# Three uses of split fp32 products in a one-core graph network: the seventh gated product, the queries, and a block of keys

## The chip, the core and the metric

The kernel runs on one core of a Trainium2 chip. A core has a matrix engine (TensorE, PE in the profile, with PEld for the loading of its stationary operand), a vector engine (VectorE, DVE), a scalar engine (ScalarE, ACT), a general engine (GpSimd, POOL) and a queue for transfers (SyncE, SP). The metric is the device time of one execution in microseconds. The kernel before takes 2311.24 us (median of three runs, 2310.18 to 2312.17).

## What is computed

The reference takes 1024 nodes of 512 features, 16384 edges sorted by target, and a condition of 16 x 256 rows. After a layer norm and a ReLU there are a batch norm, one graph convolution, four layers, a second graph convolution, and two residual sums. One layer is:

```python
a = _attn(_ln(h, ln2_w[i], ln2_b[i]), cond, Wq[i], Wk[i], Wv[i], Wo[i])
h = h + a
u = _ln(h, ln3_w[i], ln3_b[i]) @ geglu_w[i] + geglu_b[i]
val, gate = jnp.split(u, 2, axis=-1)
f = val * jax.nn.gelu(gate, approximate=False)
h = h + f @ ffo_w[i] + ffo_b[i]
```

The attention has 16 groups of 64 nodes and 8 heads of 64, with keys and values from the condition. The gated product maps 512 features to 2 x 2048, the last product 2048 back to 512. All is fp32.

## The kernel before

**Two ways of an fp32 product.** A *plain* fp32 matmul of 128 x 128 by 512 columns stands in the trace as two records. A *twelve-bit* product splits each factor into a high part, a low part and a third part (their difference), in tiles of the type fp32r; three matmuls, high x high, low x low and third x third, give the same product together, with one pass over the bank between the second and the third (multiply by 1 + 2^-12). The class `Twelve` (L366, scale at L377, copy at L382 and L384) does this for keys and values: `begin` multiplies high and low and scales, `end` multiplies the third parts and copies the bank out. `staggered` begins each unit before it ends the one before, and calls functions `beside` the units for other work.

**Seven products in place of eight.** Queries and gated products go by a scheme in which a 2 x 2 block product takes seven block products and sums of blocks. `sums_of_a` and `sums_of_b` make the sums of the factors. For the queries (`QueryQuad`, L297) all seven are plain; their sums are `weight_sums` on POOL and `sum_first` on DVE or POOL, and the sums of the results are passes of DVE (L1274). The gated product has four rounds r of four blocks c. Round 0 (`Quad`) is plain. Rounds 1 to 3 are twelve *chunks* per layer: `Chunk.steps` is a generator that a loop advances, and six of its seven products are twelve-bit (L1091). The seventh (i = 2, L1154) is two plain matmuls onto the bank of product 4.

**Splitting in the gated stage.** The right factors (rows) are split once per layer by `all_parts`, in 24 steps that `fill` places between the plain products of round 0. The left factors (weights of a chunk) arrive in two tiles, `gxa` (four blocks of 256 columns, a slot) and `gxb`, become sums on POOL (`sums`, L1071), then split: `gha`/`ghb` on ACT (L1031), `gla`/`glb` on DVE (L1033), `gsa`/`gsb` on POOL (L1037). Chunk c's last steps run among the first of chunk c + 1.

**The output stage.** `Output.unit` multiplies f (stored to memory and loaded again by `fetch`) with the last weights in 16 units, two rows of weights blocks each, two passes s over the same eight weight units. `split` splits f (ACT L314, DVE L315 and L317), `split_w` the weights (L1211, L1214, L1218), `fetch_w` loads them. In pass s = 0 blocks 0, 1, 4, 5 of h are completed, in s = 1 the others.

**Order.** Instructions go to each engine's queue by a planner that follows the order of writing. `pin` keeps the written order among pinned instructions, `in_order(engine)` chains all of one engine's instructions in a block one behind the other, `issue_after` puts a block behind one instruction, and `waiting_for(ins, engine)` makes an engine's instructions wait for `ins`. Tiles come from pools: 36 `slots` of 128 x 1024 fp32, eight banks of PSUM, six `accs`; an instruction that first writes a tile waits until a buffer is free.

**The start.** Behind a branch (`tc.If`) the root of the degrees is taken on DVE, and PE does two plain blocks of keys (`begin("k1", c, ...)`, L353) before the aggregation `agg_in` (L752), whose low rows are `hs_low` (L795). Two blocks of keys of group 1 are thus already there in layer 0.

## Time and profile before

| what | value |
|---|---|
| median of the runs | 2311.24 us (2310.18 to 2312.17) |
| profiled execution | 2311.66 us, its span 2309.9 us |
| PE busy | 2285.7 us, 99% |
| DVE, ACT, POOL busy | 1684.5 (73%), 1093.9 (47%), 646.3 us (28%) |
| granted clock of PE | 0.999 |
| layer 0, round 0 of the gated product, from 413.6 us | 34.7 us, DVE busy 32.0, POOL 4.9 |
| layer 0, the twelve chunks, from 448.3 us | 120.1 us, DVE busy 97.9, POOL 75.1 |
| layer 0, output stage, from 568.4 us | 87.1 us, DVE busy 80.7 |
| layer 1, first keys to the first scores, from 655.5 us | 49.5 us, DVE busy 31.8 |

A row of the timeline is: start, length of the group, engine, line, operation, what is written from what, shapes, count, and in brackets how long the engine stood idle before and for whom. PE's records overlap their neighbours, so the price of a matmul is the distance of the starts, not the length.

### The profile page before, as it was taken

The page shows a single profiled execution, that of the slowest core. Times are in us where ns is not written, and L with a number is a line of the kernel's source. Part 1 is how long each engine was busy: PE and PEld are TensorE (multiplying, and loading weights), DVE is VectorE, ACT ScalarE, POOL GpSimd, SP SyncE. Part 2 cuts the span into 40 slices and gives each one's busy share as a digit, 9 for nine tenths or more (in the row PEclk, how much of TensorE's full clock was granted, in tenths as well). Part 3 has the DMA queues.
Part 4 walks back from the last instruction along what each step waited for, and adds up shares of the span by engine and source line. Part 5 has one row for each costly group of instructions (what it writes and reads, how often), then busy time and mean ns, then how long its engine had stood idle before and what let it go on. Part 6 is the DMA issues. An engine that isn't in the chain of part 4 may idle for free. (4 is left out here: it accounts for less than half of the span.)

```text
span 2309.9 us, 33555 instructions
## 1 busy us (share of the span) xinstructions
PE 2285.7 (99%) x12236; PEld 1710.5 (74%) x12236; DVE 1684.5 (73%) x3111; ACT 1093.9 (47%) x2117; POOL 646.3 (28%) x575
## 2 busy tenths in 40 slices
PE   8999999999999999999999999999999999999999
PEld 4667887577877888477886888567786888667787
DVE  9876556888976556978987554988887555888965
ACT  7544445455344445455344444555335445545421
POOL 1121213274031224175022222256021123146201
PEclk9999999999999999999999999999999999999999
DMA  7042220244521101144522111033531111033551
GB/s 214 11 142 70 69 73 24 73 128 153 175 73 47 56 19 37 46 120 132 187 92 74 37 37 37 28 110 119 188 132 60 33 56 37 6 114 116 178 177 60
DMA packets 160493, 204.37 MB, mean 88 GB/s; under 512 B 11241, under 2 KB 101681, under 8 KB 160321
## 3 DMA queue, kind: packets, MB, share of 16 engines
q1 hardware_dynamic: 158224, 196.72, 26.6%
q0 software_dynamic: 1376, 4.30, 0.5%
q8 instruction: 101, 1.65, 0.3%
q10 hardware_dynamic: 720, 1.11, 0.1%
q14 instruction: 72, 0.58, 0.1%
HBM read 151.75 MB, written 50.34 MB: 87 GB/s over the span
## 5 line engine op out<-in xcount | busy, mean ns | idle before, releaser
L320 POOL TENSOR_TENSOR as_c<-ah_c,al_c 128x512 fp32r<-128x512 f32 x128 | 199.5, 1587 | 923.9 <-DVE al_c L315 482.0
L1105 ACT ACTIVATE g<-g 128x512 f32<-128x512 f32 x192 | 112.9, 588 | 193.0 <-PE g L1091 193.0
L377 ACT ACTIVATE k<-k 128x512 f32<-128x512 f32 x124 | 72.2, 585 | 225.0 <-PE k L366 223.8
L1237 PE MATMUL fy<-bh_wff,ah_f 128*128 128x512 f32 x512 | 159.2, 392 | 0.0
L1237 PE MATMUL fx<-bs_wff,as_f 128*128 128x512 f32 x512 | 157.8, 389 | 0.5 <-DVE as_f L317 0.5
L1237 PE MATMUL fy<-bl_wff,al_f 128*128 128x512 f32 x512 | 157.8, 389 | 0.0
L382 DVE COPY kT<-k 128x512 f32<-128x512 f32 x54 | 37.2, 688 | 158.4 <-PE k L366 158.4
L314 ACT ACTIVATE ah_f<-fr 128x1024 fp32r<-128x1024 f32 x64 | 67.5, 1060 | 177.0 <-PE fy L1237 112.9
L366 PE MATMUL v<-bs_wv,as_c 128*128 128x512 f32 x508 | 138.4, 394 | 3.9 <-ACT v L377 3.9
L366 PE MATMUL v<-bh_wv,ah_c 128*128 128x512 f32 x508 | 140.8, 399 | 0.0
L847 ACT ACTIVATE pr<-sc,nmax 128x256 f32<-128x256 f32 x256 | 118.0, 474 | 47.6 <-DVE nmax L842 47.1
L366 PE MATMUL v<-bl_wv,al_c 128*128 128x512 f32 x508 | 136.5, 390 | 0.0
L1091 PE MATMUL g<-gr,gsa 128*128 128x512 f32 x384 | 136.2, 436 | 0.0
L366 PE MATMUL k<-ah_c,bh_wk 128*128 128x512 f32 x496 | 133.9, 392 | 0.0
L377 ACT ACTIVATE v<-v 128x512 f32<-128x512 f32 x127 | 75.0, 591 | 122.4 <-PE v L366 122.4
L366 PE MATMUL k<-al_c,bl_wk 128*128 128x512 f32 x496 | 132.6, 389 | 0.0
L366 PE MATMUL k<-as_c,bs_wk 128*128 128x512 f32 x496 | 131.5, 396 | 0.1
L1037 POOL TENSOR_TENSOR gsa<-gha,gla 128x512 fp32r<-128x512 f32 x88 | 112.3, 1297 | 64.0 <-DVE gla L1033 64.0
L1091 PE MATMUL g<-gr,gha 128*128 128x512 f32 x384 | 120.7, 395 | 0.0
L1091 PE MATMUL g<-gl,gla 128*128 128x512 f32 x384 | 118.6, 390 | 0.0
L366 PEld LDWEIGHTS v<-bs_wv,as_c 128*128 128x128 f32 x508 | 93.8, 189 | 27.7 <-ACT v L377 5.6
L366 PEld LDWEIGHTS v<-bh_wv,ah_c 128*128 128x128 f32 x508 | 92.6, 188 | 27.9 <-issue 9.2
(326 smaller groups left out, 5542.1 us busy)
## 6 DMA issues: line engine op xcount, KB each, us to landing
f_dram<-fT SPq DMA_DIRECT2D x128, 256.0 KB, 2.7
fr<-f_dram SPq DMA_DIRECT2D x64, 512.0 KB, 4.5
ct<-cond_dram SPq DMA_DIRECT2D x48, 512.0 KB, 4.3
wff<-in_L_gnn_ffo_w_dram SPq DMA_DIRECT2D x32, 512.0 KB, 5.9
gxb<-in_L_gnn_geglu_w_dram SPq DMA_DIRECT2D x96, 128.0 KB, 2.8
gxa<-in_L_gnn_geglu_w_dram SPq DMA_DIRECT2D x96, 128.0 KB, 2.8
cond<-in_L_gnn_cond_dram SPq DMA_DIRECT2D x32, 256.0 KB, 3.8
cond_dram<-ct SPq DMA_DIRECT2D x16, 512.0 KB, 3.3
```

Of the source, the lines that this page charges most:

```text
L314: nc.scalar.mul(twelve_bits(h), x, INWARD * TINY)
L320: nc.gpsimd.tensor_tensor(twelve_bits(s)[:, k, :], h[:, k, :], l[:, k, :], OP.subtract)
L366: pin(nc.tensor.matmul(self.bank, twelve_bits(left[k // 2])[:, k % 2, self.c * P:(self.c + 1) * P], twelve_bits(right[k // 2])[:, k % 2, : ...
L377: nc.scalar.mul(self.bank, self.bank, 1.0 + TINY)
L382: nc.vector.tensor_copy(self.to(), self.bank)
L847: nc.scalar.activation(pr3[:, a, :], ps3[:, a, :], AF.Exp, bias=nmax[:, a:a + 1], accum_out=tot[:, a:a + 1])
L1037: split_left.last = pin(t.tensor_tensor(s_at, h_at, l_at, OP.subtract))
L1091: pin(nc.tensor.matmul(to, self.part(i, which)[:, k, :], self.rights[i][which].bitcast(F32R)[:, k, :], start=start and k == 0, stop=stop a ...
L1105: pin(nc.scalar.mul(to, to, 1.0 + TINY))
L1237: pin(nc.tensor.matmul(to, twelve_bits(left[which][0])[:, k, b * P:(b + 1) * P], twelve_bits(right[which])[:, k, :], start=u == 0 and whic ...
```

## The change

The seventh product of a chunk becomes twelve-bit like the others: its left block (`x[2]`, 256 columns) and its right factor are split too, its result gets its own bank (`scale_onto(2, u2)`, `end(2)`), and the sum `u2` is made before. The queries become twelve-bit products over the whole 512 rows and columns, without the seven-product scheme, in two halves of the rows: `Rows` splits four normalised blocks, `QueryWeights` the weights, `queries` gives `Twelve` units. Of the keys of group 1 one block is begun behind the branch, not two. Beside these: two right factors (`BESIDE`) give their third part to POOL; POOL's subtractions of a chunk wait for the DVE pass on the next chunk's `gla`; three chunks are loaded ahead, not two; one unit of output weights is split before the output stage, not two; `wo` is split in steps between keys; f is stored by halves of the rows, so that h is completed in the order 0 to 7; 35 slots, not 36.

```diff
-    slots = ctx.enter_context(tc.tile_pool(name="slots", bufs=36))
+    slots = ctx.enter_context(tc.tile_pool(name="slots", bufs=35))
...
+    def three_halves(name):
+        return rows.tile([P, 3 * D // 2], F32, tag="gs2", name=name, bufs=2)
...
-    f_dram = dram.tile([2, DFF // P, P, 2, 256], F32, name="f_dram")
+    f_dram = dram.tile([2, DFF // P, P, 512], F32, name="f_dram")
...
-    for c in range(2):
-        begin("k1", c, raw_wk, raw_x[0, 1])
+    with waiting_for(rsqrt.first, mybir.EngineType.PE):
+        begin("k1", 0, raw_wk, raw_x[0, 1])
...
+        yield ([high[:, c, :] for c in range(HP)], [low[c // 2][:, c % 2, :] for c in range(HP)],
+               third)
...
+            yield
...
+            yield
...
-    SPLIT = (0, 5, 6, 4, 1, 3)
-    EARLY = (0, 1, 4, 6, 5, 3)
+    SPLIT = (0, 5, 6, 4, 1, 3, 2)
+    EARLY = (0, 1, 4, 6, 5, 3, 2)
+    BESIDE = (4, 6)
...
+    def right_beside(name, x, h, s):
+
+        low = slot(f"gl_{name}")
+        nc.scalar.mul(h.bitcast(F32R), x, INWARD / TINY)
+        less = [t512(f"gt_{name}_{k}") for k in range(2)]
+        for k in range(2):
+            nc.scalar.mul(less[k], h[:, k, :], TINY)
+        for k in range(2):
+            yield low
+            pin(nc.vector.scalar_tensor_tensor(low.bitcast(F32R)[:, k, :], x[:, k, :], 1.0 / TINY,
+                                               h[:, k, :], OP.mult, OP.subtract))
+            pin(nc.gpsimd.tensor_tensor(s.bitcast(F32R)[:, k, :], low[:, k, :], less[k],
+                                        OP.subtract))
+
...
-        pin(nc.scalar.mul(h.bitcast(F32R), x, INWARD * TINY))
-        yield
-        pin(nc.vector.scalar_tensor_tensor(l.bitcast(F32R), h, -1.0 / TINY, x, OP.mult, OP.add))
-        yield
+        yield pin(nc.scalar.mul(h.bitcast(F32R), x, INWARD * TINY))
+        split_left.low = pin(nc.vector.scalar_tensor_tensor(l.bitcast(F32R), h, -1.0 / TINY, x,
+                                                            OP.mult, OP.add))
+        yield split_left.low
...
-            if c % 2 == 0:
-                tag = ("row", "last")[c // 2]
-                Chunk.room = rows.tile([P, D], F32, tag=tag, name=f"gy_{self.n}")
-            self.last = columns_of(Chunk.room)[:, c % 2]
+            self.x.append(rows.tile([P, M], F32, tag="gy", name=f"gy_{self.n}", bufs=2))
...
             if low:
-                to = [t512(f"g{n}b_{self.n}") for n in "hls"]
+                last = three_halves(f"gs2_{self.n}")
+                all_to = [[t512(f"g{n}b_{self.n}") for n in "hls"],
+                          [last[:, i * M:(i + 1) * M] for i in range(3)]]
             else:
-                to = [flat(slot(f"g{n}a_{self.n}")) for n in "hls"]
-            self.parts[low] = [columns_of(t.bitcast(F32R)) for t in to]
-            yield from split_left(self.x[low], *to, t)
-
+                all_to = [[flat(slot(f"g{n}a_{self.n}")) for n in "hls"]]
+            flows = []
+            for i, to in enumerate(all_to, int(low)):
+                self.parts[i] = [columns_of(t.bitcast(F32R)) for t in to]
+                flows.append(split_left(self.x[i], *to, t))
+            for flow in flows:
+                next(flow)
+            yield
+            while flows:
+                flow = flows.pop(0)
+                if next(flow, None):
+                    flows.append(flow)
+                    yield
...
+            add(u2, d, u2)
             self.scale_onto(3, u3)
+            self.scale_onto(2, u2)
...
-            for k in range(2):
-                pin(nc.tensor.matmul(d, self.last[:, k, :], self.rights[2][:, k, :], start=False,
-                                     stop=k == 1, skip_group_check=True))
+            d = self.end(2)
...
-            add(d, d, u2)
...
+                nc.sync.dma_start(f_dram[s, self.r * KC + c], self.tiles[c][:, s, :])
...
+        def split(self, n, t=nc.vector):
...
+                self.f[n] = left_parts([self.raw.pop(n)], f"f_{self.l}_{n}", t)
...
-                    to = h[4 * (b // 2) + 2 * s + b % 2]
+                    to = h[4 * s + b]
...
+    class Rows:
+
+        def __init__(self, l, half, x):
+            self.x, self.n, self.parts = x, f"ln2_{l}_{half}", [[], [], []]
+
+        def high(self, i):
+            for n, part in zip("hls", self.parts):
+                part.append(slot(f"b{n}_{self.n}_{i}"))
+            nc.scalar.mul(twelve_bits(self.parts[0][i]), self.x[i], INWARD / TINY)
+
+        def low(self, i):
+            (h, l, _), x = (t[i] for t in self.parts), self.x[i]
+            for k in range(2):
+                nc.vector.scalar_tensor_tensor(twelve_bits(l)[:, k, :], x[:, k, :], 1.0 / TINY,
+                                               h[:, k, :], OP.mult, OP.subtract)
+
+        def third(self, i):
+            h, l, s = (t[i] for t in self.parts)
+            for k in range(2):
+                nc.vector.scalar_tensor_tensor(twelve_bits(s)[:, k, :], h[:, k, :], -TINY,
+                                               l[:, k, :], OP.mult, OP.add)
...
+    class QueryWeights:
+
+        def __init__(self, l, x):
+            high = four_wide(f"ah_wq_{l}")
+            self.x, self.l = x, l
+            self.parts = [[high[:, :2, :], high[:, 2:, :]], [], []]
+
+        def high(self, i):
+            for n, part in zip("ls", self.parts[1:]):
+                part.append(slot(f"a{n}_wq_{self.l}_{i}"))
+            nc.scalar.mul(twelve_bits(self.parts[0][i]), self.x[i], INWARD * TINY)
+
+        def rest(self, i):
+            (h, l, s), x = (t[i] for t in self.parts), self.x[i]
+            nc.vector.scalar_tensor_tensor(twelve_bits(l), h, -1.0 / TINY, x, OP.mult, OP.add)
+            for k in range(2):
+                nc.gpsimd.tensor_tensor(twelve_bits(s)[:, k, :], h[:, k, :], l[:, k, :],
+                                        OP.subtract)
+
+    def queries(l, half, wq, rows, by):
+
+        to = blocks_in(qTs, half, f"qT_{l}_{half}")
+        return [Twelve(f"q_{l}_{half}_{c}", wq.parts, c, rows.parts, to(c), by[c % 2])
+                for c in range(KC)]
...
+        wq = QueryWeights(l, wq)
...
         else:
-            scale_first(1, deviations(mv_first[1], "ln2_0_4"))
-            with waiting_for(scale_first.last, mybir.EngineType.Pool):
-                wq = weight_sums(wq, "wqs_0")
+            root = deviations(mv_first[1], "ln2_0_4")
+            for i in range(2):
+                wq.high(i)
+                with waiting_for(rsqrt.last, mybir.EngineType.Pool):
+                    wq.rest(i)
...
+        def split_first(i):
+            first_rows.high(i)
             with in_order(mybir.EngineType.DVE):
-                turn_first(l, half[1][:2], ((1, 1),))
+                first_rows.low(i)
+                if l:
+                    first_rows.third(i)
...
+        def split_wq(i):
+            wq.high(i)
+            with in_order(mybir.EngineType.DVE):
+                wq.rest(i)
+
+        def staggered_queries(half, rows, beside):
+            staggered(queries(l, half, wq, rows, (1, 0)), beside)
...
-                staggered(units, {1: lambda: first(0, 1), 2: lambda: first(2, 3), 4: turn_some,
-                                  6: lambda: to_scale[0](0, 1), 7: turn_more})
+                staggered(units, {0: lambda: split_wq(0), 1: lambda: first(0, 1),
+                                  2: lambda: first(2, 3), 3: lambda: split_wq(1), 4: turn_some,
+                                  5: lambda: split_first(0), 6: lambda: split_first(1),
+                                  7: lambda: to_scale[0](0, 1)})
+                staggered_queries(0, first_rows, {
+                    0: lambda: (to_scale[0](2, 3), turn_more(*half[1][:2])),
+                    1: lambda: (turn_more(*half[1][2:]), begin_more(), more_rows.high(0)),
+                    2: lambda: (finish_more(0), more_rows.high(1)),
+                    3: lambda: finish_more(1)})
...
-            staggered(units, {2: turn_some, len(units) - 1: lambda: turn_first(0, range(4, 8))})
-            sum_first(nc.gpsimd, 0)
-            sum_first(nc.gpsimd, 1)
+            with in_order(mybir.EngineType.Activation), in_order(mybir.EngineType.DVE):
+                staggered(units, {2: turn_some, 3: lambda: split_first(0),
+                                  4: lambda: (split_first(1), first_rows.third(0),
+                                              first_rows.third(1), scale_first(1, root))})
+                staggered_queries(0, first_rows, {
+                    1: lambda: (turn_more(*range(4, 8)), begin_more(), more_rows.high(0)),
+                    2: lambda: (finish_more(0), more_rows.high(1)),
+                    3: lambda: finish_more(1)})
...
+        split_cond(l, 1)
+        staggered_queries(1, more_rows, {})
...
+            wo_flow = out_parts(l, wo) if not g else iter(())
+            wo = next(wo_flow, wo)
...
-            k = keys(l, g + 1, wk, 2 if l == 0 and g == 0 else 0)
+            k = keys(l, g + 1, wk, 1 if l == 0 and g == 0 else 0)
...
+                next(wo_flow, None)
...
+                if i in BESIDE:
+                    flow = right_beside(name, x, high, mid)
+                    Chunk.rights[i] = high, next(flow), mid
+                    yield
+                    for _ in flow:
+                        yield
+                    continue
...
+        def begin_split(n, low, t=nc.gpsimd):
+            flow = ready[n].split_steps(low, t) if n < len(ready) else iter(())
+            next(flow, None)
+            return flow
+
+        first_chunk = []
+
+        def fill_first():
+            for flow in first_chunk.pop(0):
+                next(flow, None)
...
-                first_chunk = split_first()
-            q.rest((lambda: next(first_chunk.pop(0), None)) if c == KC - 1 else fill)
+                long, short = (begin_split(0, low) for low in (False, True))
+                first_chunk.extend([[parts], [long] * 3, [short], [short] * 4, [], []])
+            q.rest(fill_first if c == KC - 1 else fill)
...
+        def split_rest(short):
+            long = begin_split(0, False)
+            next(long, None)
+            with waiting_for(split_left.low, mybir.EngineType.Pool):
+                for flow in short, long:
+                    for _ in flow:
+                        pass
...
-                if n > 0:
+                if 0 < n < 5:
...
-                if before:
-                    chunk.split(True, nc.gpsimd)
+                for _ in islice(short, 2):
+                    pass
...
-                    split(0, False)
+                    split_rest(short)
                     load()
+                for _ in parts:
+                    pass
...
-                    output.split(0)
+                    with in_order(mybir.EngineType.Activation), in_order(mybir.EngineType.DVE), \
+                            in_order(mybir.EngineType.Pool):
+                        output.split(0, nc.gpsimd)
                     output.fetch(1)
...
-                    if step == 0 and n >= 0 and n % KC == 0:
-                        next(ahead)
...
+                short = begin_split(0, True)
+                if n == 0:
+                    next(ahead)
+        output.fetch_w(1)
         output.fetch_w(2)
-        output.fetch_w(3)
...
-            half = [0, 1, 4, 5], [2, 3, 6, 7]
+            half = range(4), range(4, 8)
...
-                output.fetch_w(n + 4)
+                output.fetch_w(n + 3)
```

160 lines of the change are left out of this document (41 added, 119 removed).

## Prediction

> **What bounds the kernel now.** I read the page first, then what TensorE (PE) waited for, then PE's timeline stage by stage, and last the other engines beside it.
>
> ```profile
> span 2309.9 us, 33555 instructions
> ...
> PE 2285.7 (99%) x12236; PEld 1710.5 (74%) x12236; DVE 1684.5 (73%) x3111; ACT 1093.9 (47%) x2117; POOL 646.3 (28%) x575
> ...
> PEclk9999999999999999999999999999999999999999
> ```
>
> PE is busy in 2285.7 of 2309.9 us, at full granted clock. Of the 24 us left these waits of PE (total, times, longest) are those that the change can touch:
>
> ```profile
> PE v L366 <- ACT v L377: 3.9, 4, 2.5
> ...
> PE begun_k L353 <- DVE v_deg L151: 1.7, 1, 1.7
> PE g L1091 <- DVE g L1109: 1.3, 4, 0.3
> ```
>
> The rest is the start, before the first matmul has data. So the time is what PE has to stream, plus any new idle. VectorE (DVE) at 73% is an average and says nothing of a stage. Two prices carry the sum, both from PE's timeline (start, length of the group, what, how many records):
>
> ```profile
> 145.84 1.88 PE L297 MATMUL qb<-ln2S,wqs 128*128 128x512 f32 x4
> ...
> 163.01 1.91 PE L201 MATMUL tr_cond<-ident,cond 128*128 128x128 f32 x16
> ...
> 470.04 1.88 PE L1154 MATMUL g<-ln3T,gy 128*128 128x512 f32 x4
> ...
> 479.97 1.88 PE L1154 MATMUL g<-ln3T,gy 128*128 128x512 f32 x4
> ...
> 655.52 1.07 PE L366 MATMUL k<-ah_c,bh_wk 128*128 128x512 f32 x4
> ...
> 665.49 1.07 PE L366 MATMUL v<-bh_wv,ah_c 128*128 128x512 f32 x4
> ```
>
> From 145.84 to 163.01 us ten query products of four records each ran back to back: 17.17 / 10 = 1.717 us for a product, which is two plain fp32 matmuls over 512 columns. From 655.52 to 665.49 eleven groups of four twelve-bit matmuls ran: 9.97 / 44 = 0.2266 us each. From one L1154 to the next is one gated chunk: 9.93 us.
>
> **The change part by part.**
>
> *Seventh gated product.* Per chunk two plain matmuls (1.717) become six twelve-bit ones (6 x 0.2266 = 1.360). PE saves 0.357 us per chunk; 3 rounds x 4 chunks x 4 layers = 48 chunks: -17.1 us. A chunk then takes 9.57 us, if the other engines keep up. One chunk of layer 0 on DVE, POOL and ScalarE (ACT), and each engine's busy time in it:
>
> ```profile
> 489.58 1.75 DVE L1033 SCALAR_TENSOR_TENSOR gla<-gha,gxa 128x1024 fp32r<-128x1024 f32 x1 [0.77 <-ACT gha L1031]
> ...
> 495.21 0.69 DVE L1109 SCALAR_TENSOR_TENSOR g<-g,gs 128x512 f32<-128x512 f32 x1
> ...
> 570.13 1.22 DVE L315 SCALAR_TENSOR_TENSOR al_f<-ah_f,fr 128x1024 fp32r<-128x1024 f32 x1
> ...
> 488.96 1.29 POOL L1037 TENSOR_TENSOR gsb<-ghb,glb 128x512 fp32r<-128x512 f32 x1 [1.96 <-DVE glb L1033]
> 491.41 2.55 POOL L1037 TENSOR_TENSOR gsa<-gha,gla 128x512 fp32r<-128x512 f32 x2 [1.16 <-DVE gla L1033]
> 493.92 0.74 POOL L1071 TENSOR_TENSOR gxa<-gxa,gxb 128x256 f32<-128x256 f32 x1
> 494.74 1.44 POOL L1071 TENSOR_TENSOR gxa<-gxa 128x256 f32<-128x256 f32 x2
> ...
> 498.43 1.04 ACT L1031 ACTIVATE gha<-gxa 128x1024 fp32r<-128x1024 f32 x1
> ...
> 489.90:499.80 9.90, 9.90 (x41) 7.51 (x40) 8.01 (x12) 6.25 (x11) 6.75 (x8) 1.00 0.35 106
> ...
> 413.60:448.30 34.70, 34.70 (x82) 14.72 (x80) 31.99 (x50) 16.39 (x23) 4.92 (x7) 1.00 0.23 69
> ```
>
> DVE gains one pass from a bank (0.69) and a 256-wide low part (0.4, estimated from half of a 512-wide pass). It loses a block: `gla` took 1.75 us where it began at 489.58 while POOL's `gsb` ran until 490.25; a 1024-wide pass of the same kind without POOL is 1.22 (`al_f`, in the output stage). The new order lets POOL start only behind it. So 8.01 + 1.1 - 0.5 = 8.6 of 9.57 us. A weight step (`wff`) is in that sum, which the last three chunks no longer have. POOL gains a 256-wide subtraction: 6.75 + 0.74 = 7.5 of 9.57; ACT gains some 0.4 on 6.25. No bound there by busy time.
>
> The right factor of the seventh product is split in the quads' stage (last row: 34.70 us, DVE busy 31.99, POOL 4.92). Two of the seven factors give their third part to POOL, so the steps between the products stay 24, and DVE's passes in them stay 24. Four POOL passes of 1.29 can block DVE there, 5.2 us at the very most, against 2.7 us idle; and the first chunk's third parts leave DVE for POOL, three passes, 2 us. I cost it at nothing; without that cover it is at most 0.5 us per layer. In the chunk that ends a layer the last product waits for a bank's pass with nothing between; PE waits there 0.3 us now (1.3 over four layers, above), and I leave it.
>
> *Queries.* Per layer 7 products x 2 x 1.717 = 24.0 us become 2 halves x 4 blocks x 12 x 0.2266 = 21.8: -2.3. What they need now comes out of a longer chain for each half of the rows: turned (ACT and DVE), high part (ACT), low and third parts (DVE). Layer 1:
>
> ```profile
> 668.22 1.91 PE L201 MATMUL tr_ln<-ident,xn_ln 128*128 128x128 f32 x16
> ...
> 668.86 2.65 DVE L812 TENSOR_SCALAR ln2T<-tr_ln,cols 128x128 f32<-128x128 f32 x8 [7.42 <-PE tr_ln L201]
> ...
> 675.40 0.16 DVE L1333 SCALAR_TENSOR_TENSOR less_ln<-mv,y_ln 128x4 f32<-128x4 f32 x1
> ...
> 672.05 0.63 ACT L377 ACTIVATE v<-v 128x512 f32<-128x512 f32 x1
> ...
> L314 ACT ACTIVATE ah_f<-fr 128x1024 fp32r<-128x1024 f32 x64 | 67.5, 1060 | 177.0 <-PE fy L1237 112.9
> ...
> 96.55 1.28 DVE L338 SCALAR_TENSOR_TENSOR bs_wk<-bh_wk,bl_wk 128x512 fp32r<-128x512 f32 x2
> ...
> 705.02 1.96 PE L835 MATMUL sc<-kT,qT 64*64 64x256 f32 x32
> ```
>
> PE's transposes end at 669.9 and ten groups of 0.907 follow: the first query starts at about 679.0. ACT has turned by 672.05; in its fixed order come two scales and two copies (0.6 each, as in that row) beside the two high parts (1.06 each, the mean of `ah_f` on the page): 677.2. DVE ends the second half's root at 675.6 and makes low and third parts, eight passes of 0.64 (as `bs_wk`): 680.7; PE wants the low ones from 679.9 to 680.8 and the third ones from 682.7. That fits, and the second half has seven groups, 6.3 us, of the first one before it. So -2.3 in each of layers 1 to 3, -6.8 (bounds: 0 to +1 us of idle in each). Layer 0 has less cover:
>
> ```profile
> 85.39 7.11 PE L353 MATMUL begun_k<-ct,wk 128*128 128x512 f32 x16 [1.71 <-DVE v_deg L151]
> 91.93 0.79 PE L752 MATMUL agg_in<-high,c 128*128 128x512 f32 x1
> ...
> 88.31 2.08 DVE L795 SCALAR_TENSOR_TENSOR hs_low<-hs_in,y_deg,high 128x512 fp32r<-128x512 f32 x3 [0.92 <-ACT high L794]
> ...
> 129.07 1.91 PE L201 MATMUL tr_ln<-ident,xn_ln 128*128 128x128 f32 x16
> ...
> 129.71 3.38 ACT L814 ACTIVATE ln2T<-tr_ln,cols 128x128 f32<-128x128 f32 x8 [0.26 <-PE tr_ln L201]
> ...
> 126.67 1.91 DVE L189 TENSOR_SCALAR xn_ln<-hall,mv_first,y_ln 128x512 f32<-128x512 f32 x4
> ```
>
> There five units stand before the queries, not eight. After the transposes (130.8) PE has seven groups, until 137.1. ACT turns until 133.1; behind two scales, a high part and a copy its second high part ends at 138.0: PE stops 0.5 us in the first query. DVE goes on with six passes of 0.64 and the four normalised blocks of the second half (1.91, put behind them now), so that their transposes end 0.7 late; its two copies and eight turning steps reach 148.1, a high part and a scale on ACT 149.8, where PE wants that scale at 148.6; the same again for the next block. Together 0.5 + 0.7 + 1.2 + 1.2, some 3.5 us of idle, estimated (0 to 5).
>
> *One begun block, not two.* From 85.39 eight records fewer, 3.4 us. The aggregation then wants its first low row, which DVE has at 88.31 + 0.7 = 89.0 where PE is free at 88.8: -3.2. The block comes back as twelve matmuls: +2.7. They stand between the first two scores of layer 0, in front of the place where PE lost the 2.5 us above (an ACT scale queued behind softmax work that DVE brought late); that cover takes most of it: -2.0 (0 to -2.5). The steps of `wo`'s split between the keys are the same instructions: nothing (or the other 1.4 us of that row). Layer 0 in sum: -2.3 + 3.5 - 3.2 + 2.7 - 2.0 = -1.3.
>
> *Output stage.* Only the first of eight units of weights is split before the stage, not two; the second has to be made during the first unit (24 x 0.2266 = 5.44 us):
>
> ```profile
> 568.05 1.02 PE L1237 MATMUL fy<-bh_wff,ah_f 128*128 128x512 f32 x2
> ...
> 569.47 0.75 DVE L1160 SCALAR_TENSOR_TENSOR fT<-g,gcols,g 128x512 f32<-128x512 f32 x1
> ...
> 572.53 0.68 DVE L1214 SCALAR_TENSOR_TENSOR bl_wff<-wff,bh_wff 128x512 fp32r<-128x512 f32 x1
> ...
> 574.58 0.69 DVE L1218 SCALAR_TENSOR_TENSOR bs_wff<-bh_wff,bl_wff 128x512 fp32r<-128x512 f32 x1
> ```
>
> Now DVE makes here, between the last `fT` and 575.3, the weights of the unit after next; then they are those of the next. The first matmul of the stage begins to stream when the last plain one is through, 568.46; unit 1 at 573.9, and it wants its last third part at 575.0. The chunk in front ends 1.3 us sooner after its gates, which brings DVE some 0.4 later against PE: 0.3 to 0.7 us of idle, four times, +2.0 (0 to +4). From there DVE has 5.1 us of work per 5.44 and gains. On SP the weight loads keep their place behind the last stores; `f` stored in rows of 512, not twice 256, and the other order of the blocks of `h` move no work.
>
> **Sum.** -17.1 - 6.8 - 1.3 + 2.0 = -23.2, against the profiled execution (2311.66 us; span 2309.9): 2288.5. The median of the runs shown is 0.4 below that execution: 2288.
>
> **The rivals.**
>
> *POOL's chain paces the chunk.* From one `gla` to the next the new order runs `gsb` 1.29, the new subtraction 0.74, `gsa` 2.55, three sums (493.92 to 496.18) 2.26, `gha` 1.04, `gla` 1.22: 9.1 us, some 9.4 with the hand-overs (0.08 us from 491.33 to 491.41), against 9.57. If `gla` is blocked again it is 10.0: eleven steps fall 4.7 us behind, of which 2.3 are cushion (`gsa` is ready that much before PE wants it). Four layers give back 4 x 2.4 = 10 us: 2298. For it speaks how near 9.4 is; against it that POOL stands idle before each `gsb` now. The Trainium skill, "SBUF — State Buffer", Who interferes with whom, has a DVE instruction with two SBUF inputs and a POOL one that reads SBUF exclude each other for the whole instruction. By that rule, with which 1.75 against 1.22 agrees, POOL too can be blocked by `glb`, and the chain is 10.0.
>
> *Slower: the split chain of the rows is not covered.* ACT's fixed order holds a query block's scale behind the turning and the high part of the next half. Per layer turning 3.4, two high parts 2.1 and four low passes 2.6 make 8.1 us; exposed once in each layer, 32 us less the 3.5 counted: 2317. The sign turns at (23.2 + 3.5) / 4 = 6.7 us per layer. Against it: nine microseconds of units stand in front in layers 1 to 3.
>
> *Every wait goes.* Layer 0 without idle and without the 2.5 (-5.3), the other 1.4 and the 1.3 gone, nothing lost in Output: -17.1 - 6.8 - 5.3 - 2.7 = -32: 2280.
>
> *PE waits for room instead* (35 slots, not 36, with three more held by the seventh factor and one more chunk loaded ahead): the 17.1 come back as waits, 2305. I count 34 slots held in a chunk, so it is near, but fits.
>
> *A plain pass costs as much as a twelve-bit one.* Then a plain matmul is 4 x 0.2266 = 0.906 us, not 0.858, and the change saves two passes per chunk and 16 per layer: 21.8 + 14.5 = 36 us where the rows give 26; 2278. The Trainium skill, "FP8 and Floating Point Precision", TensorE Precision Notes, counts four passes for true fp32. The rows contradict only the price of a pass, but that price is measured.
>
> **How the numbers follow.** As summed 0.70; POOL's chain 0.12; every wait gone 0.04; room 0.05, half of it within 0.2%; slower 0.08; passes 0.01. 0.2%, 4.6 us, is about what a measurement of this kernel can tell from no change. Faster 0.70 + 0.12 + 0.04 + 0.01 + 0.03 = 0.90, same 0.02, slower 0.08. The likeliest one's own range is 2281 to 2295 (its unknown terms all at their good or bad ends). The range, 2280 to 2303, takes in POOL's chain and every wait gone.
>
> **What would show it.** Chunks 9.5 to 9.6 us apart without PE waits; `gla` at 1.2 us, begun before POOL's subtractions; from layer 1's first key to its first score 46.5 to 48 us (49.5 now); PE waits on ACT's `q` in layer 0 alone; a PE wait of 0.3 to 0.7 us on DVE's `bs_wff` at each Output stage. Wrong would make it: PE waits on POOL's `gsa` that grow from chunk to chunk, waits on ACT's `q` in every layer, or a chunk above 9.7 us.

## The result and the profile after

The changed kernel takes 2304.30 us (median of 19 runs, 2301.61 to 2308.55), beside 2311.51 us of the kernel before (19 runs, 2310.16 to 2312.26): a ratio of 0.9971 (95% interval 0.9964 to 0.9978). It is faster by 7.2 us; the forecast was 23. The profiled execution of it was its slowest run, 2308.55 us.

The page of the kernel after, its span and its busy times, and then what PE waited for (total us, times, longest), the rows that are new or have grown:

```profile
span 2306.8 us, 34462 instructions
...
PE 2271.7 (98%) x12496; PEld 1757.1 (76%) x12496; DVE 1738.5 (75%) x3172; ACT 1169.6 (51%) x2245; POOL 750.3 (33%) x647
```

```profile
PE v L370 <- ACT v L381: 7.2, 5, 2.2
PE gc L301 <- DVE gu L982: 4.4, 8, 0.7
...
PE k L370 <- ACT k L381: 1.7, 1, 1.7
...
PE fy L1252 <- DVE bl_wff L1229: 0.8, 2, 0.4
```

PE is busy 14 us less, where 26 us of products were taken away, and stands idle 11 us more. (Time at half clock counts as busy, and so do gaps of less than 0.16 us: a record lasts 0.39 us, and its neighbour begins 0.227 us on.) Where, the stages tell. Layer 1 of the kernel before, then of the kernel after: from the first keys to the first scores, to the quads, to the chunks, to the output stage, to the next keys. Columns: window, its length, busy time of PE, PEld, DVE, ACT and POOL with their records, granted clock, DMA.

```profile
655.52:705.02 49.50, 49.50 (x185) 31.81 (x184) 31.84 (x76) 26.24 (x45) 10.99 (x8) 1.00 0.14 48
705.02:946.32 241.30, 240.51 (x1729) 190.89 (x1729) 148.02 (x322) 118.92 (x280) 55.07 (x40) 1.00 0.11 36
946.32:980.93 34.61, 34.61 (x81) 14.70 (x80) 31.47 (x50) 16.38 (x23) 5.19 (x7) 1.00 0.23 69
980.93:1100.70 119.77, 119.43 (x483) 90.02 (x481) 97.44 (x132) 66.03 (x110) 74.98 (x76) 1.00 0.43 130
1100.70:1188.16 87.46, 87.46 (x386) 72.24 (x385) 81.07 (x105) 27.39 (x28) 8.84 (x4) 1.00 0.51 172
```

```profile
654.69:702.29 47.60, 47.60 (x226) 39.01 (x224) 33.14 (x67) 34.27 (x59) 11.09 (x8) 1.00 0.03 6
702.29:944.36 242.07, 240.25 (x1729) 190.92 (x1729) 147.97 (x322) 122.58 (x284) 54.74 (x40) 1.00 0.13 43
944.36:980.18 35.82, 34.70 (x82) 14.66 (x80) 33.38 (x49) 18.52 (x26) 17.09 (x15) 1.00 0.31 96
980.18:1096.76 116.58, 116.27 (x507) 94.20 (x505) 106.39 (x149) 69.31 (x119) 90.53 (x88) 1.00 0.35 112
1096.76:1185.36 88.60, 88.20 (x386) 71.76 (x384) 82.56 (x107) 29.45 (x30) 8.91 (x4) 1.00 0.53 190
```

The queries gained 1.9 us and the chunks 3.2; the attention lost 0.8, the quads' stage 1.2 and the output stage 1.1. One boundary needs care: in the kernel before, the last product of the chunks is plain, and the next stage's first record begins some 0.4 us before PE is through with it (its first pair takes 0.85 us, after the change 0.46). So the chunks gained 3.6, and the output stage lost 1.5.

The same for all layers, each stage from its first PE record to that of the next, in us. A stretch of 3.4 us at half the granted clock that fell into a stage, 1.7 us of time, is taken out (below):

| stage | before | after | forecast | measured, all layers |
|---|---|---|---|---|
| layer 0, start to aggregation | 87.9 | 85.0 | -3.2 | -2.9 |
| layer 0, first keys to first scores | 43.1 | 44.9 | +1.2 | +1.8 |
| layer 0, first scores to quads | 247.1 to 248.8 | 248.5 | +0.7 | -0.4 to +1.3 |
| layers 1 to 3, first keys to first scores | 49.5 | 47.6 | -6.8 | -5.7 |
| layers 1 to 3, first scores to quads | 241.3 | 242.1 to 242.7 | 0 | +3.1 |
| quads | 34.6 | 35.8 | 0 | +4.8 |
| chunks (boundary put right) | 120.2 | 116.6 | -17.1 | -14.4 |
| output (boundary put right; times of layers 0 to 2) | 87.1 | 88.2 to 88.6 | +2.0 | +5.7 |
| sum | | | -23.2 | -8.0 to -6.3 |

The two ends in the row of layer 0 are because a stretch of half clock fell into a wait of PE there, where it cost less than 1.7. The fastest runs differ by 8.6 us, the medians by 7.2. The rest is such stretches, of which the kernel after has more: the granted clock is 1.0 in its six fastest runs and 0.998 in its slowest.

**Half clock after a wait.** Two neighbouring windows of the kernel after in layer 3's output stage, columns as above:

```profile
2220.30:2223.70 3.40, 2.03 (x7) 0.83 (x6) 2.45 (x2) 0.53 (x1) 0.00 (x0) 1.00 1.12 410
2223.70:2227.10 3.40, 3.40 (x9) 2.66 (x9) 2.21 (x2) 1.06 (x1) 0.00 (x0) 0.51 1.04 377
```

In the first PE stood idle 1.4 of 3.4 us; in the next it had half its clock. The profiles of this study (before, after and 18 others) hold 21 such stretches inside the work, and in the 3.413 us in front of every one PE stood idle for 1.3 to 2.3 us. Not each such wait has one, and most of that is a matter of position: in each profile the stretches begin whole multiples of 3.413 us apart. Cut the traces, from 25 us on, into windows on that grid: all 14 windows with 1.9 us of idle time or more were followed by a stretch, 7 of the 68 with 1.3 to 1.9 us were, and none with less. A wait that two windows share counts in neither in full. The profiled run of before held one, that of after three. So a wait of this size can cost 1.7 us more than it shows. The Trainium skill, "TensorE: Matmul & The Clock Gate", What's actually happening, has the clock halved after an idle window of about 3.4 us; the length agrees (3.413 us in each), but here 1.4 us of idle time in such a window were enough.

### The profile page after: what moved, and what is told of

The parts are those of the page before. It is cut to its first block, busy times and chain, and to the rows that moved or that the text cites. A ratio compares the mean times of both kernels' runs of the same rounds, so it can differ in the third digit from the quotient of the medians.

```text
span 2306.8 us, 34462 instructions
## 1 busy us (share of the span) xinstructions
PE 2271.7 (98%) x12496; PEld 1757.1 (76%) x12496; DVE 1738.5 (75%) x3172; ACT 1169.6 (51%) x2245; POOL 750.3 (33%) x647
## 5 line engine op out<-in xcount | busy, mean ns | idle before, releaser
L1050 POOL TENSOR_TENSOR gsa<-gha,gla 128x512 fp32r<-128x512 f32 x96 | 124.2, 1315 | 40.2 <-DVE gla L1045 40.2
L1109 PE MATMUL g<-gr,gsa 128*128 128x512 f32 x384 | 120.0, 394 | 0.0
L1252 PEld LDWEIGHTS fy<-bl_wff,al_f 128*128 128x128 f32 x512 | 96.3, 188 | 24.5 <-DVE bl_wff L1229 3.7
```

Source lines behind the costliest of these rows:

```text
L1050: split_left.last = pin(t.tensor_tensor(s_at, h_at, l_at, OP.subtract))
L1109: pin(nc.tensor.matmul(to, self.part(i, which)[:, k, :], self.rights[i][which].bitcast(F32R)[:, k, :], start=start and k == 0, stop=stop a ...
L1252: pin(nc.tensor.matmul(to, twelve_bits(left[which][0])[:, k, b * P:(b + 1) * P], twelve_bits(right[which])[:, k, :], start=u == 0 and whic ...
```

## Experiments

Each is the changed kernel with the edit shown. All were timed beside the kernel before on the same chip; the stages, from the profile of each, tell more than the medians, which differ by 1.7 us with each stretch of half clock. Stage times below are those of layer 1.

**The quads' stage.** PE waits there for the bank's pass `gu`. DVE, POOL and PE of the kernel after, layer 0:

```profile
426.32 1.17 DVE L1037 SCALAR_TENSOR_TENSOR gl<-ln3T,gr 128x512 fp32r<-128x512 f32 x1
427.41 0.68 DVE L982 TENSOR_TENSOR gu<-gc,gu 128x512 f32<-128x512 f32 x1
428.01 1.15 DVE L1017 SCALAR_TENSOR_TENSOR gr<-ln3S,gt 128x512 fp32r<-128x512 f32 x1
...
425.35 4.95 POOL L1039 TENSOR_TENSOR gr<-gl,gt 128x512 fp32r<-128x512 f32 x3 [1.73 <-DVE gl L1037]
...
428.14 1.98 PE L301 MATMUL gc<-ln3S,wgate 128*128 128x512 f32 x4 [0.43 <-DVE gu L982]
```

A DVE pass with both inputs in SBUF takes 1.15 to 1.17 us while POOL makes third parts, in place of 0.68; the pass on the bank `gc`, between them, still takes 0.68. By the Trainium skill, "SBUF — State Buffer", Who interferes with whom, a DVE instruction with two SBUF inputs contends with a POOL one that reads SBUF, and one with at most one such input, outside the fast modes that use two ports, does not; these rows agree.

`e1_pool_out` gives these two factors' third part to ACT, as a copy:

```diff
-            pin(nc.gpsimd.tensor_tensor(s.bitcast(F32R)[:, k, :], low[:, k, :], less[k],
-                                        OP.subtract))
+            pin(nc.scalar.mul(s.bitcast(F32R)[:, k, :], less[k], -1.0))
```

> The changed kernel, but the two right factors that gave their third part to POOL get it as a scaled copy by ACT: four POOL passes of 1.3 to 1.7 us per layer are gone, and DVE's passes stay as they are. It leaves out the subtraction of the low part in these third parts, so its values are not the reference's. Theory A (POOL's passes lengthen the DVE passes that run beside them, from 0.68 to 1.17 us, and PE waits for the bank's pass gu behind them): the quads' stage goes from 35.8 back to 34.6 to 34.9 us in each layer, 4 to 5 us in all. Rival B (the seventh factor alone makes DVE late in this stage, with or without POOL): the stage stays at 35.6 to 35.8, the time within 1 us of the changed kernel.

Measured: 2302.51 us, ratio 0.9960 (0.9946 to 0.9974), the stage 35.5 to 35.8 us. Theory A's number missed. But the edit was not clean: DVE now stands idle for ACT, which has the copies to make, and the second wait (0.9 us) is one beside POOL's sums of the second chunk:

```profile
956.48 0.69 DVE L1017 SCALAR_TENSOR_TENSOR gr<-ln3S,gt 128x512 fp32r<-128x512 f32 x1 [0.64 <-ACT gt L1015]
```

`e9_sums` moves those sums back behind the stage; `e10_dve_sums` also leaves all third parts to DVE:

```diff
             if c == 2:
-                sum_chunk(1)
                 load()
+        sum_chunk(1)
         sum_chunk(2)
...
-    BESIDE = (4, 6)
+    BESIDE = ()        # e10 only
```

> The changed kernel with the four POOL sums of the second chunk moved back behind the quads' stage, where they stood before; the four POOL third parts stay. Theory A (any POOL pass that runs beside DVE's splitting lengthens DVE's passes; the third parts make the first of the two waits for the bank's pass gu, the second chunk's sums the second): the first wait, 0.4 to 0.7 us, stays, the second one falls from 0.7 to about 0.2, the stage from 35.8 to 35.2 to 35.4 us. Rival B (the seventh factor's passes on DVE alone): no change, 35.8.

> The same, and no right factor gives its third part to POOL: DVE makes them, with the last steps of the seventh factor left to the first chunk. Theory A (POOL beside DVE): POOL does only the first chunk's sums in the stage, as before, so the stage is back at 34.6 to 34.8 us in each layer, 4 to 5 us less in all than the changed kernel, if the first chunk hides the passes left over; otherwise up to 1 us of them comes back there. Rival B (DVE has too many passes in the stage): 35.8 or more, because DVE now has the four third parts too.

Measured: 2306.05 us, 0.9977 (0.9968 to 0.9987), and 2309.90 us, 0.9992 (0.9982 to 1.0001). Quads and chunks of layer 1, of e9 and of e10:

```profile
942.56:977.84 35.28, 34.71 (x82) 14.67 (x80) 32.85 (x49) 18.51 (x26) 12.57 (x11) 1.00 0.31 97
977.84:1095.33 117.49, 116.80 (x506) 94.04 (x505) 107.19 (x149) 69.19 (x119) 94.17 (x92) 1.00 0.35 111
```

```profile
943.43:978.04 34.61, 34.61 (x82) 14.71 (x80) 31.72 (x49) 18.59 (x26) 6.46 (x7) 1.00 0.26 84
978.04:1097.12 119.08, 117.32 (x506) 93.86 (x505) 111.44 (x153) 69.15 (x119) 95.75 (x92) 1.00 0.35 112
```

DVE has 49 passes in the stage in all three kernels (50 before the change), so their number is not what differs. Their length is: beside 17.1 us of POOL they take 33.4 us and the stage 35.8, beside 12.6 they take 32.9 and the stage 35.3, beside 6.5 they take 31.7 and the stage 34.6, as before the change. Theory A holds for the stage, but POOL's sum is not its measure: with 10.4 us of POOL e1 takes 35.6, and with 9.6 `e18_b2` (below) takes 34.6. It counts which passes POOL lies beside. And the chunks' stage takes 0.9 and 2.5 us longer in e9 and e10: what was put off has no cover there either. `e18_b2` puts off two steps, with their third parts on POOL: quads 34.6, chunks 1.1 longer than with the same edits without it. Both stages together (quads over 34.6, chunks over those of the kernel that lacks only this edit), the seventh factor's passes cost 1.2 us per layer in the kernel after, 1.6 in e9, 2.5 in e10 and 1.1 in e18; no place that was tried hides them.

**The edge for POOL's third parts in the chunks.** `e7_nowait`:

```diff
-            with waiting_for(split_left.low, mybir.EngineType.Pool):
-                for flow in short, long:
-                    for _ in flow:
-                        pass
+            for flow in short, long:
+                for _ in flow:
+                    pass
```

> The changed kernel without the edge that holds POOL's third parts of a chunk until DVE's pass on the next chunk's gla is through. Theory A (that pass is held up by POOL again, 1.7 us in place of 1.2, but DVE has 0.9 us to spare per chunk): chunks stay 9.56 us apart and the stage at 116.5 to 116.7 us. Rival B (POOL's chain sets the pace in the last chunks, where PE already waits 0.1 to 0.3 us for gsa): the waits grow, and the stage takes 1 us or more longer. Rival C (the edge itself makes gsa late): the waits for gsa go, 0.5 us less per layer.

Measured: 2301.82 us, 0.9961 (0.9946 to 0.9976); the chunks take 115.8 us, 0.8 less in every layer. That is the gain of rival C, but the wait is another one, as the rows show. DVE's low passes in the chunks (durations in ns: least, median, most), of the kernel after and of e7:

```profile
L1045 DVE SCALAR_TENSOR_TENSOR gla<-gha,gxa x48: 1211/1224/1808, 446.3 to 2143.2; 128x1024 fp32r<-128x1024 f32 x48
L1045 DVE SCALAR_TENSOR_TENSOR glb<-ghb,gxb x48: 674/971/1451, 448.1 to 2150.3; 128x512 fp32r<-128x512 f32 x48
L1045 DVE SCALAR_TENSOR_TENSOR gs<-gs,gy x48: 409/954/966, 450.0 to 2150.9; 128x256 fp32r<-128x256 f32 x48
```

```profile
L1045 DVE SCALAR_TENSOR_TENSOR gla<-gha,gxa x48: 1212/1758/2314, 445.3 to 2137.3; 128x1024 fp32r<-128x1024 f32 x48
L1045 DVE SCALAR_TENSOR_TENSOR glb<-ghb,gxb x48: 673/679/1450, 447.1 to 2144.5; 128x512 fp32r<-128x512 f32 x48
L1045 DVE SCALAR_TENSOR_TENSOR gs<-gs,gy x48: 409/413/962, 449.0 to 2145.1; 128x256 fp32r<-128x256 f32 x48
```

The edge does free `gla`, by 0.53 us. It puts the same block on `glb` (0.29) and `gs` (0.54), and it holds POOL back. In the kernel after, POOL's sums for the next chunk come later from chunk to chunk, ACT's high part `gha` waits for them (0.03 us early in layer 1, 1.08 in the row below; in e7 never), and PE waits for the scale of a bank that stands behind it on ACT:

```profile
1069.19 1.06 ACT L1044 ACTIVATE gha<-gxa 128x1024 fp32r<-128x1024 f32 x1 [1.08 <-POOL gxa L1081]
...
1072.32 0.60 ACT L1123 ACTIVATE g<-g 128x512 f32<-128x512 f32 x1
...
1072.96 0.73 PE L1109 MATMUL g<-gr,gsa 128*128 128x512 f32 x2
```

PE had used this `gsa` since 1067.78, so it is not `gsa` that is late. From `gla` to `gla` POOL, ACT and DVE take 9.6 to 9.8 us in the middle of the stage, and PE's chunks are 9.56 us apart eight times and then 9.69, 9.87 and 9.63, which makes 0.5 us; the other 0.3 us is a longer wait in front of the layer's last product. In e7 all eleven distances are 9.56.

**The output stage.** DVE, layer 1, kernel after; PE begins the stage at 1096.76 and its second unit at 1102.2:

```profile
1101.71 0.69 DVE L1233 SCALAR_TENSOR_TENSOR bs_wff<-bh_wff,bl_wff 128x512 fp32r<-128x512 f32 x1
...
1104.93 1.23 DVE L319 SCALAR_TENSOR_TENSOR al_f<-ah_f,fr 128x1024 fp32r<-128x1024 f32 x1 [1.20 <-ACT ah_f L318]
...
1107.40 0.69 DVE L1229 SCALAR_TENSOR_TENSOR bl_wff<-wff,bh_wff 128x512 fp32r<-128x512 f32 x1
```

DVE is late for the second unit, and then, idle 1.2 us for a part of f, late for the third too (0.95 us lost at 1108.7, with the slow records that follow a wait). `e4_fetch` loads that part earlier; `e12_units` makes three steps of the second unit's weights in the last chunks:

```diff
         output.fetch_w(1)
+        output.fetch(2)
...
-                output.fetch(n + 2)
+                output.fetch(n + 3)
```

```diff
+                if n == 3:
+                    output.fetch_w(1)
...
-                if 0 < n < 5:
+                if n > 0:
                     next(ahead)
...
-        output.fetch_w(1)
         output.fetch_w(2)
```

> The changed kernel with the load of the third f unit put on SP's queue in front of the last chunk's stores of f, and each later one a unit earlier. Theory A (DVE idles 1.2 us at the output stage's second unit because that load stands behind stores that wait for the last chunk's gates): the waits at the third unit, about 0.9 us in each layer, go: 3 to 4 us less; those at the second unit, 0.5 us, stay. Rival B (the load is not what makes DVE late; one unit of weights fewer split ahead of the stage does it all): the stage stays 1.5 us longer than before and the time within 1 us.

> The changed kernel with three of the five steps of a second unit of output weights made ahead of the output stage, in the last chunks. Theory A (DVE starts the stage with al_f, as_f and four weight passes in front of it, 5.1 us, at 98.4 where PE wants the second unit at 102.2): the waits at the second unit, about 0.5 us, and at the third, about 0.9 us, go, 88.5 to 87.1 us in each layer, 5 us in all. Rival B (the load of f is what makes the third unit late): 0.5 us go, 0.9 stay, 2 us in all. Rival C (the passes moved make the last chunks late): no gain.

Measured: e4 2303.52 us, 0.9967 (0.9954 to 0.9979), the stage 87.95 us, 0.6 less: the third unit's wait is gone, as theory A has it, and a new one of 0.3 us, for `as_f`, comes near the end of the stage. e12 2299.84 us, 0.9948 (0.9931 to 0.9964), the stage 87.3 and 87.1 us in the layers, as before the change, and the chunks no longer: theory A, all of it.

**The attention, layers 1 to 3.** PE waits 1.5 us for ACT's scale of v in each first group; before it was 0.5. SP's rows for wo, of before and of after, and what SP waited for in that stretch after:

```profile
687.11 1.22 SPq L125 DMA_DIRECT2D wo<-in_L_gnn_Wo_dram  x2
```

```profile
699.72 0.90 SPq L126 DMA_DIRECT2D wo<-in_L_gnn_Wo_dram  x2
```

```profile
SPq L126 <- PE q L370: 58.8, 1, 58.8
```

wo is loaded 12.6 us later, when the last query matmuls give slots free. Its split (2 us of ACT, 5 of DVE), which before lay under the queries, now lies behind the first scores. What is late for it is the second softmax, into which a pass for the residual has come:

```profile
725.94 0.82 ACT L1556 ACTIVATE again<-x_again,x_shift,x_root 128x512 f32<-128x512 f32 x1
...
728.44 0.63 ACT L381 ACTIVATE v<-v 128x512 f32<-128x512 f32 x1
```

`e2_wo` makes the split in one go; `e11_woearly` also takes the slots of wo earlier; `e15_x` was to move the residual's rows by two groups; `e19_xlate` does it with edges:

```diff
             wo = next(wo_flow, wo)
+            for _ in wo_flow:        # e2, e11
+                pass
...
         split_cond(l, 1)
+        wo = load_w(Wo[l], f"wo_{l}")        # e11
         staggered_queries(1, more_rows, {})
         qT = [qTs.pop(i) for i in range(2)]
-        wo = load_w(Wo[l], f"wo_{l}")
...
-            if g in (1, 2):        # e15: (3, 4) at both places, rows counted from there
...
-                base_of(2 * l + g - 1)
+                with waiting_for(scores.last, mybir.EngineType.Activation), \
+                        behind_on(scores.last, mybir.EngineType.DVE):        # e19
+                    base_of(2 * l + g - 1)
```

> The changed kernel with wo split in one go ahead of the second group's keys, as before, not in steps between them. Theory A (the steps, some 6 us of DVE work now behind the first scores, push the residual's passes into the second group's softmax, and ACT's scale of v comes late): PE's wait for ACT's scale of v in the first group falls from about 1.5 to 0.5 us in layers 1 to 3, 3 us less in all. Rival B (the scores come 2.9 us earlier against a DVE chain that does not): the wait stays at 1.3 to 1.6 us and the time within 1 us.

> The changed kernel with the slots of wo taken, and its load issued, ahead of the second half's queries, and wo split in one go. Theory A (wo's load waits for slots that the last queries hold, 12.6 us later than before; its split, 2 us of ACT and 5 us of DVE, then falls behind the first scores, and either ACT's scale of k or that of v comes late, so that moving the split alone gained nothing): the sum of the waits for ACT's k and v in the first group falls by 0.7 to 1.2 us in layers 1 to 3, about 3 us in all. Rival B (the scores themselves come earlier against DVE): less than 1 us in all.

> The changed kernel with the residual's rows (load, one ACT pass and two DVE passes each) two groups later in every layer. Theory A (DVE's chain in the first group is late because wo's split, whose load waits for the queries' slots, now stands in it; the residual's passes stand right in front of the second softmax): taking 1.4 to 2.4 us of other work out of that chain brings ACT's scale of v forward, and the wait in the first groups of layers 1 to 3 falls from 1.5 to 0.5 us or less: 2.5 to 4 us in all. Rival B (the scores themselves set the softmax, nothing in front of it counts): the wait stays. Rival C (the passes make another group late): the wait moves there.

> The changed kernel with edges that hold the residual's ACT pass and two DVE passes of each row until the softmax of the third or the fourth group is through (the edit before this one had left them where they were, in front of the second group's softmax and in it). Theory A (DVE's and ACT's chain in the first group is late through what stands in it besides the softmax): ACT's scale of v comes forward, the wait in the first groups of layers 1 to 3 falls from 1.5 to 0.2 to 0.7 us, 2.5 to 4 us less in all than the changed kernel. Rival B (the scores set the softmax): the wait stays at 1.4 us or more.

Measured, with the stage from first scores to quads (242.1 us in the kernel after, 241.3 before):
- e2: 2304.78 us, 0.9971 (0.9961 to 0.9981), 242.1 us. The wait for v fell to 0.5, and one of 0.6 for k came.
- e11: 2307.81 us, 0.9980 (0.9971 to 0.9990), 241.0 us. PE's wait for v is back at 0.4 to 0.5, as before the change, but the second half's queries end 1.3 us later, behind ACT's scale of `q`. Theory A for the wait; nothing gained.
- e15: 2303.36 us, 0.9971 (0.9958 to 0.9984), 242.1 us. The edit left the passes where they were (one ACT pass at 714.8, the other at 723.9, between the softmax's), so it tells nothing.
- e19: 2301.10 us, 0.9953 (0.9938 to 0.9968), 241.1 us in each of the three layers, 1.0 to 1.6 less. Theory A: the residual's passes in front of the softmax and in it. PE's waits for v, all layers (the edit moves the lines by 11), 7.2 us in the kernel after:

```profile
PE v L381 <- ACT v L392: 2.4, 5, 0.8
```

`e13_room` asks whether one slot more would have done: `slots` 36, not 35, `work` 8 tiles, not 10.

> The changed kernel with 36 slots, as before, and 8 working tiles of 512 in place of 10 to pay for them. Theory A (loads come late for want of a slot: wq in layer 0, wo in each): wq and wo land earlier, the wait for ACT's first scale of k in layer 0 (1.7 us) and the one for ACT's v in the first groups of layers 1 to 3 (1.5 us each) shrink by half or more: 2 to 5 us less than the changed kernel. Rival B (one slot more does not help, because the queries hold all that is freed): those waits stay, under 1 us. Rival C (the tiles taken away are missed where factors are split): the quads' stage or the chunks grow by 1 us or more per layer.

Measured: 2313.12 us, 1.0011 (1.0002 to 1.0020). The wait for k falls to 0.3 us, those for v stay. In layer 0 the attention takes 8.7 us more, because PE's transposes of the condition now wait for its loads, which go into working tiles: none of the three as worded, and nearest to rival C, in another stage than it named. At these numbers the working tiles are scarcer than the slots.

**Layer 0.** ACT and PE of the kernel after:

```profile
123.10 1.06 ACT L1294 ACTIVATE ah_wq<-wq 128x1024 fp32r<-128x1024 f32 x1 [17.32 <-DMA wq<-in_L_gnn_Wq_dram]
...
125.29 1.06 ACT L381 ACTIVATE k<-k 128x512 f32<-128x512 f32 x2
...
126.02 0.70 PE L370 MATMUL k<-as_c,bs_wk 128*128 128x512 f32 x2 [1.74 <-ACT k L381]
```

The scale that PE waits for, ready at 124, stands on ACT behind the two high parts of wq, and those behind wq's load. `e3_wq` puts them behind the first two scales (`split_wq_0(i)` holds the body of the old loop); `e6_two` begins two blocks of keys again:

```diff
-            for i in range(2):
-                wq.high(i)
...
-                staggered(units, {2: turn_some, 3: lambda: split_first(0),
+                staggered(units, {0: lambda: split_wq_0(0), 1: lambda: split_wq_0(1),
+                                  2: turn_some, 3: lambda: split_first(0),
```

```diff
-        begin("k1", 0, raw_wk, raw_x[0, 1])
+        for c in range(2):
+            begin("k1", c, raw_wk, raw_x[0, 1])
...
-            k = keys(l, g + 1, wk, 1 if l == 0 and g == 0 else 0)
+            k = keys(l, g + 1, wk, 2 if l == 0 and g == 0 else 0)
```

> The changed kernel, but in layer 0 the two high parts of wq stand on ACT behind the scales of the first two units of keys, not in front of them. Theory A (ACT, in a fixed order, waits for the load of wq until 123.1 us and the scale of the first key block stands behind it): PE's new wait of 1.7 us at 124 us goes, 1.5 to 1.9 us less. Rival B (wq is then late for the queries or for the turning of the rows): the wait comes back at the first queries, less than 0.5 us gained.

> The changed kernel with two blocks of keys begun behind the branch, not one. Theory A (the forecast's terms: eight records and their cover at the start, twelve matmuls in front of PE's wait for ACT's v in the first group of layer 0): the aggregation begins 3.2 to 3.4 us later, and from the first score of layer 0 to the quads it takes 0.5 to 1 us less, because the wait for v grows from 1.8 to about 4 us: 2.4 to 2.9 us slower than the changed kernel. Rival B (the wait for v hangs on PE's own work and does not grow): the stage takes 2.7 us less, and the whole is 0.5 to 0.7 us slower.

Measured: e3 2303.45 us, 0.9971 (0.9958 to 0.9983). The wait for k is gone, but another comes in front of the queries, of 1.4 us here, in e14, e16 and e18, and 0.6 in e17 and e20:

```profile
134.17 1.20 PE L370 MATMUL v<-bs_wv,as_c 128*128 128x512 f32 x4 [1.40 <-ACT v L381]
```

First keys to first scores takes 43.5 us in e3 without its stretch of half clock and 43.6 to 44.4 in the five other profiles with this edit; in the 12 of the kernel after and of other edits it takes 44.1 to 45.0, and the wait for k is 0.3 to 1.9. So theory A has the wait for k right, but the gain is some 0.8 us on average and not 1.5 to 1.9, because a wait comes back later: a part of rival B.

e6 2305.25 us, 0.9974 (0.9964 to 0.9984): the aggregation begins 3.4 us later, and first scores to quads takes 2.8 us less. (First keys to scores takes 44.0, as it does without this edit in e7, 44.1.) That makes 0.6 us more, rival B's number, where the forecast's terms made it 2.5. PE's waits for v:

```profile
PE v L370 <- ACT v L381: 5.2, 4, 2.0
```

They are less than in the kernel after, not more. That wait comes behind the second scores, and the reading that fits, though no run shows it by itself, is that work in front of these delays the softmax as much as PE.

**Together.** `e14_units_wq` joins e12 and e3; `e16_three` adds e7; `e17_four` adds e15's edit; `e18_b2` sets `BESIDE = (2,)` in place of `(4, 6)`; `e20_best` is e18 with e19's edges in place of e15's edit.

> The changed kernel with both edits that gained: three steps of a second unit of output weights ahead of the output stage, and the high parts of wq behind the first two scales. Theory A (two waits in different stages, which add): 1.2 to 1.7 us less than with the output weights alone, 2298 to 2299. Rival B (what is won at the start of layer 0 is lost at the next wait there, for ACT's scale of v): as the output weights alone, 2300.

> Output weights, wq's high parts, and no edge for POOL's third parts, together on the changed kernel. Theory A (three waits in three stages, which add): 5.6, 1.2 and 3 us less than the changed kernel's stages, a time of 2295 to 2296. Rival B (without the edge the output weights' passes in the last chunks are late, or the reverse): 2297 to 2299.

> The same, and the residual's rows two groups later. If all four waits add, 2292 to 2294; if moving the rows gains nothing, 2295 to 2296, as without it. In both cases the 1.2 us per layer of the quads' stage are still in it, and so are the short stretches at half the clock.

> The same as the last, but of the right factors the seventh gives its third part to POOL, not the fifth and the seventh product's neighbours; its last two steps fall into the first chunk. Theory A (the seventh factor's passes have no room in the quads' stage: beside POOL they cost 1.2 us there, and put off they cost at least as much in the first chunk): the quads' stage falls by 0.6 to 1.2 us and the chunks' stage grows by as much or more, the time within 2 us. Rival B (DVE's and POOL's passes do find room in the first chunk): the stage falls and the chunks stay, 3 to 4 us less.

> All that gained, together: three steps of a second unit of output weights ahead, wq's high parts behind two scales, no edge for POOL's third parts, only the seventh's own right factor with its third part on POOL, and the residual's passes held back. If the waits add, 2292 to 2294; if the residual's passes gain nothing, 2296 to 2297.

Measured: 2298.71 us, 0.9946 (0.9933 to 0.9960); 2297.57, 0.9939 (0.9924 to 0.9954); 2298.20, 0.9942 (0.9928 to 0.9955); 2296.90, 0.9937 (0.9922 to 0.9952); 2293.24, 0.9918 (0.9905 to 0.9932). e14 has theory A's time, though its stage from first keys to first scores gains only 0.5 us on e12's. In e16 rival B came: the chunks are 9.56 us apart again, but PE waits longer in front of the layer's last product, and the stage takes 116.2 us, against 116.3 with the edge (e14) and 115.8 in e7:

```profile
1090.80 0.72 PE L1109 MATMUL g<-gr,gsb 128*128 128x512 f32 x2 [0.50 <-DVE g L1127]
```

e17 adds e15's edit and tells as little. e18's stages shift by 1.2 and 1.1 us (theory A). In e20 the waits add as expected; it beats both kernels, 17.8 us under the before of its chip.

## Why the prediction was wrong

**Right: the prices of PE's work.** Third parts of the seventh product of two neighbouring chunks (kernel after) begin 9.56 us apart; forecast 9.57. With the edge gone (e7) the whole stage gains 4.4 us per layer with the boundary put right, as forecast (4.3).

```profile
993.01 0.63 PE L1109 MATMUL g<-gr,gs 128*128 128x512 f32 x2
...
1002.57 0.63 PE L1109 MATMUL g<-gr,gs 128*128 128x512 f32 x2
```

The queries of layers 1 to 3 gained 1.9 of 2.3 us without a wait on ACT's `q`, and the aggregation began 2.9 of 3.2 us earlier. Of the rivals, the split chain of the rows did not break through. POOL's chain did fall behind PE, as that rival had it, but by 0.03 to 0.27 us per chunk, and its delay reached PE only after eight chunks, through ACT's scales and not through `gsa`: 0.5 us per layer, not 2.4, and the edge made it (e7).

**Wrong: the covers.** Of 23.2 us forecast, 7.2 came. The quads' stage (4.8 us), the output stage (3.7 more than its term), the attention of layers 1 to 3 (3.1) and the chunks (2.7) make up 14.3 of what is missing. In the order of the steps:
- "I cost it at nothing" (the seventh factor's split in the quads' stage): +4.8 us, 1.2 per layer, where even the bound given for it was 0.5. What failed is the use of a stage's idle sum as cover: PE waits for one pass `gu`, and the passes in front of that one were lengthened. The second chunk's sums, a fourth of POOL's time there, were not counted at all (e9, e10).
- "It loses a block" (-0.5 us of DVE per chunk for `gla`): the block moved to `glb` and `gs`, and the edge that moved it cost PE 0.8 us per layer (e7).
- "0.3 to 0.7 us of idle, four times" in the output stage: the second unit cost 0.5 in layer 1, as forecast, but the stages 1.2 to 1.5 each. "From there DVE has 5.1 us of work per 5.44 and gains" is the step that failed: DVE was held up by a load of f and was late for the third unit as well (e4, e12).
- "The steps of `wo`'s split between the keys are the same instructions: nothing": +3.1 us in layers 1 to 3. The queries' slots moved wo's load and its split behind the scores (e11, e19). The rival of the 35 slots looked for PE waiting in the chunks; the want of slots showed as late loads elsewhere. That the measured time is near that rival's 2305 is luck.
- Layer 0: "that cover takes most of it: -2.0" was nothing (e6), and the queue of ACT behind wq's load, a wait of 1.7 us, was not seen (e3). The first is a wait that moves along with PE's work. The 3.5 us of idle time forecast for the queries of layer 0 did not come in that size either: PE's rows there are 0.4 us for `q` and 0.3 for v. So +1.8 us from first keys to first scores is near the forecast's +1.2 by luck.

What stays open: why, of the windows with 1.3 to 1.9 us of idle time, a few are followed by half the clock and most are not, and where the last 0.4 us per layer of the queries went.

## What to carry to other kernels

Cover is no sum over a stage: for each wait, ask which one instruction ends it, and what runs beside or in front of that one. When an engine is given work beside another, count the passes of the two that have two inputs in SBUF as slower, and when an edge moves a block, look for the pass that has it next, and for what the engine that it holds back does later. When tiles are held longer, follow the queue of loads that waits for them into the next stage; and put a wait off by moving what stands in front of its releaser, not what stands in front of the waiting engine.

## What was not expected of the hardware

- PE's clock fell to half for 3.41 us only behind waits: 21 stretches in 20 profiles, each behind a window of 3.413 us with 1.3 to 2.3 us of idle time, on a grid that does not move within a profile. A gain in waits is worth up to 1.7 us more than the wait.
- A wait costs more than its row: the records behind it come 0.33 to 0.39 us apart, not 0.227, for some four matmuls (0.4 us of the 0.95 lost at 1108.7 in the kernel after). The rows of the waits in the output stages add up to 2.1 us, the stages lost 5.7.
- With 1.15 to 1.17 us for 0.68, a DVE pass with two SBUF inputs loses some 0.5 us beside POOL, and a pass that reads a bank loses none.
